# Wq's third row group by GpSimd's queue into the room of the first, Wk's second half in its place on the other two queues

## The chip, the core and the metric

The kernel runs on one core of a Trainium2 chip. The metric is the device time of one launch in microseconds, as the median of three runs. A core has five engines that matter here, each with an instruction queue that is worked off in order: TensorE (PE in the profile, with its weight loads as PEld), VectorE (DVE), ScalarE (ACT), GpSimd (POOL) and SyncE (SP), which only issues transfers. ScalarE and GpSimd can issue transfers (DMAs) as well. All arithmetic is in float32.

## The reference, cut to what matters

There are 32 graphs of 512 nodes with 512 features each, and two layers:

```python
h = relu(layernorm(x))                       # layer 0
agg = (adj @ h) / max(rowsum(adj), 1e-6)
x = x + relu(concat([h, agg]) @ W.T)
h = relu(layernorm(x))                       # layer 1
q, k = split(h @ Wqk, 2); v = h @ Wv
agg = adj @ (k * mask)
w = mask * sum(q * agg, -1) / sqrt(512)
x = x + softmax(w over the nodes)[:, None] * v
```

For layer 1, q is only ever multiplied with an aggregate of k. So the kernel computes the 512 x 512 product M = Wq Wk^T once, at its start, and uses h M in place of q and k. The change concerns how Wq and Wk, the two halves of `Wqk`, get into the core for this product.

## The kernel before, in words

The graphs are worked through one after the other in a loop; TensorE's 512 x 512 products are made with seven block products in place of eight (the lists `LEFT`, `RIGHT` and `ORDER`). The order of all instructions on each engine is written out by hand: the text of the kernel is the order of the queues (`tc.manual_schedule`), and a `Plan` says after which block product of TensorE other work is put.

The function `start` prepares the weights and the first graph. TensorE needs Wq and Wk transposed, and this is done in two steps. `exchange` loads a group of rows with four DMAs, one for each 32 partitions (in the order of `TURNS`), so that blocks of 32 x 32 come to lie in the right partitions; DVE's 32 x 32 transposition then does the rest (`turn_ordered` at line 769 for Wq, `turn_natural` at line 776 for Wk's first two groups, and a transposition written out at line 921 for Wk's second half). With `two_queues` the four DMAs of a group go by turns to SyncE's and ScalarE's queue; GpSimd issues none in `start`.

The pieces are:

- Wq comes in four groups of rows, `ask_wq(0)` to `ask_wq(3)`, each of 256 KB in four DMAs of 64 KB. Each lands in a room of its own in `sq`, a part of the tile `mv`, and `turn_wq(d)` transposes it into column d of `wqT` (a part of the tile `late`).
- Wk comes in two single groups, `ask_wk(0)` and `ask_wk(1)`, and its second half at once, `ask_wk(2, 2)`, in four DMAs of 128 KB. They land in `sk` and are transposed into `wkT`.
- `multiply(d, b, n)` is TensorE's part: row group d of Wq with n groups of Wk from b on. TensorE does them in the order (0, 0), (0, 1), (1, 0, 2), (2, 0, 2), then (0, 2, 2), (1, 2, 2), (2, 2, 2), and (3, 0, 2) and (3, 2, 2) around the first transpositions of the normalised x. Their rows carry the name `pm` and line 893.

DVE's order in `start` is: Wq's first rows, Wk's first and second group, Wq's second rows, Wq's third rows, Wk's second half in two pieces, Wq's fourth rows, and then the statistics of the first graph's x (line 266), each power of which is taken by GpSimd (line 272). GpSimd's own order before that is a few constants and `make_identity` (lines 197 and 199 of masks.py). Line 726 is GpSimd's only DMA in the kernel before: two loads of 512 KB for each graph that add to what lies there (names `tv<-dx`). In the profile the transfers of Wqk are `mv<-in_L_gnn_Wqk_dram`.

Of the kernel before, what the change touches and what calls it, by code (L numbers as in the profile page):

```python
# [22 lines left out]
def kernel(  # L23
# [11 lines left out]
    nc = tc.nc  # L35
# [181 lines left out]
    one_queue, two_queues = (nc.sync, nc.sync), (nc.sync, nc.scalar)  # L217
# [9 lines left out]
    def exchange(src, name, t=None, queues=one_queue):  # L227


        if t is None:  # L230
            t = big.tile([P, 8, P], F32, tag="s", bufs=2, name=name)
        for q in TURNS:
            queues[q // 2].dma_start(
                out=t[q * R:(q + 1) * R, :, :], in_=src[:, :, ts(q, P)].rearrange("k r j -> r k j")
            )
        return t
# [530 lines left out]
    def turn_ordered(t, d, dst, a, b):  # L767

        nc.vector.transpose(
            dst[:, a:b, ts(d, P)].rearrange("p a (k r) -> p k a r", r=R),  # L770
            t[:, :, a * R:b * R].rearrange("p k (a r) -> p k a r", r=R),
        )

    def turn_natural(t, h, dst, a, b):

        nc.vector.transpose(
            dst[:, a:b, ts(h, P)].rearrange("p a (k r) -> p k a r", r=R),
            t[:, :, a * R:b * R].rearrange("p k (a r) -> p k a r", r=R),
        )
# [37 lines left out]
    def start():  # L817
# [13 lines left out]
        def rows16(n):  # L831
            return room[:, n:n + 2048].rearrange("p (k f) -> p k f", f=P)

        sq, sk, s1 = rows16(0), rows16(2048), rows16(7168)
        wk_rows = weight_source(wqk[:, F:2 * F])
        wq_rows = wqk[:, 0:F].rearrange("(q c r) j -> c q r j", q=Q, c=C)
        def ask_wq(d):
            exchange(wq_rows[d], f"swq_{d}", sq[:, 4 * d:4 * d + 4], two_queues)

        def ask_wk(b, n=1):  # L840
            exchange(wk_rows[4 * b:4 * (b + n)], f"swk_{b}", sk[:, 4 * b:4 * (b + n)], two_queues)

        ask_wq(0)
        ask_wk(0)
        ask_wk(1)
        ask_wq(1)
        ask_wq(2)
        ask_wk(2, 2)
        ask_wq(3)
        room_x(0)  # L850
# [15 lines left out]
        wqT = late[:, 0:2048].rearrange("p (c f) -> p c f", c=C)  # L866
# [39 lines left out]

        def turn_wq(d, pieces=1):
            for a in range(pieces):
                turn_ordered(sq[:, 4 * d:4 * d + 4], d, wqT, 4 // pieces * a, 4 // pieces * (a + 1))

        def turn_wk(b, pieces=1):
            for a in range(pieces):
                turn_natural(sk[:, 4 * b:4 * b + 4], b, wkT, 4 // pieces * a, 4 // pieces * (a + 1))

        turn_wq(0)
        turn_wk(0, 2)
        turn_wk(1, 2)
        turn_wq(1, 2)
        turn_wq(2)
        for a in range(2):  # L920
            nc.vector.transpose(
# [159 lines left out]
        f = F1[0] = FrontH1(0)  # L1081
# [58 lines left out]
    }  # L1140
    with tc.manual_schedule(engines=engines):
        weights, mvR = start()
        post = None
        for i in range(1, B):
            more, last = i + 1 < B, i + 1 == B
            f = F1[i] = FrontH1(i)
# [240 lines left out]
```

## Time and profile before

| what | value |
|---|---|
| median of three runs | 2258.78 us (2258.16 to 2259.42) |
| profiled execution | 2258.43 us |
| its span, first to last instruction | 2256.7 us |
| instructions | 32841 |
| PE busy | 2251.1 us, 100% of the span |
| DVE busy | 1915.2 us, 85% |
| ACT busy | 1027.5 us, 46% |
| POOL busy | 176.1 us, 8% |
| data moved | 463.68 MB, 205 GB/s in the mean |

The profile is of one execution. "Busy" is the time in which at least one instruction of the engine ran. In lists of instructions a row gives the start and the length in us, the engine, the line of the kernel, the operation, the tile written and those read, how many instructions the row joins (x2), and in square brackets how long the engine was idle before them and what ended that: another engine's instruction, a DMA, or "issue" where the profile shows no cause. The chain of waits follows the work that ended last back to its start.

### The profile page before, as it was taken

Reading aid. Unit: us, or ns where it says so; the run is one execution under the profiler, and the core shown is the slowest. Engines: PE = TensorE matmul, PEld = TensorE weight load, DVE = VectorE, ACT = ScalarE, POOL = GpSimd, SP = SyncE. Lnnn points to the kernel's source line nnn. Section 1 sums busy time; section 2 is a strip of 40 time slices with the busy share of each in tenths; the row PEclk is TensorE's granted clock in tenths of the full one; section 3 lists DMA queues with packets and bytes.
Section 4 is the critical chain, followed back from the end, with each engine's and each line's share of the span. In section 5 each row is a group of like instructions: output and inputs, shape, how many; then the busy total and the mean of one; then the engine's idle time right before and its main releaser. Section 6 shows DMA issues by size and latency. Waiting matters only on the chain.

```text
span 2256.7 us, 32841 instructions
## 1 busy us (share of the span) xinstructions
PE 2251.1 (100%) x10532; PEld 1982.1 (88%) x10532; DVE 1915.2 (85%) x3786; ACT 1027.5 (46%) x1897; POOL 176.1 (8%) x261
## 2 busy tenths in 40 slices
PE   9999999999999999999999999999999999999999
PEld 7888888888888888888888888888888888888888
DVE  7998888888888888888888888888888888888787
ACT  5454443455434444434454344544444543445324
POOL 0000000000000000000001100000000000000000
PEclk9999999999999999999999999999999999999999
DMA  8878777777777786777777777777768777787543
GB/s 222 259 222 246 213 209 199 199 212 225 204 206 191 210 234 197 212 190 204 232 209 210 197 196 219 221 205 200 197 212 228 203 211 192 204 235 203 157 125 109
DMA packets 409150, 463.68 MB, mean 205 GB/s; under 512 B 37745, under 2 KB 271345, under 8 KB 404754
## 3 DMA queue, kind: packets, MB, share of 16 engines
q1 hardware_dynamic: 396914, 427.31, 63.7%
q0 software_dynamic: 8928, 32.51, 8.7%
q10 hardware_dynamic: 3136, 1.77, 0.3%
q8 instruction: 83, 1.36, 0.3%
q14 instruction: 89, 0.73, 0.1%
HBM read 293.93 MB, written 167.51 MB: 204 GB/s over the span
## 4 chain that ended last, share of the span: by engine, by line
PE 99%; DMA 0%; ACTq 0%; DVE 0%; issue 0%; DVEq 0%
PE ptv L498 28%; PE pp_o L105 20%; PE pp_y L105 10%; PE pp_u L105 10%; PE pq_o L105 10%; PE pq_y L105 5%; PE pr_o L105 5%; PE pq_u L105 5%; PE pr_u L105 2%; PE pr_y L105 2%; PE pw L549 1%; DMA mv<-in_L_gnn_Wqk_dram 0%; PE pm L893 0%; PE pp_t L105 0%; PE pp_v L105 0%; PE pq_v L105 0%
## 5 line engine op out<-in xcount | busy, mean ns | idle before, releaser
L498 PE MATMUL ptv<-mv,h1T 128*128 128x256 f32 x2842 | 618.1, 379 | 0.0
L498 PEld LDWEIGHTS ptv<-mv,h1T 128*128 128x128 f32 x2842 | 540.2, 190 | 73.2
L76 DVE TENSOR_TENSOR tv<-tv 128x256 f32<-128x256 f32 (+1 forms) x645 | 322.0, 511 | 13.2 <-ACT tv L82 1.5
L82 ACT ACTIVATE tv<-ptv 128x512 f32<-128x512 f32 (+1 forms) x360 | 185.2, 542 | 266.7 <-PE ptv L498 266.7
L105 PE MATMUL pp_u<-h1m,aT 128*128 128x256 f32 x1024 | 241.9, 379 | 0.0
L105 PE MATMUL pp_y<-wide 128*128 128x256 f32 x992 | 234.5, 379 | 0.0
L105 PE MATMUL pp_o<-y,aT 128*128 128x256 f32 x992 | 234.3, 379 | 0.0
L105 PE MATMUL pp_o<-w,wide 128*128 128x256 f32 x960 | 226.8, 379 | 0.0
L105 PEld LDWEIGHTS pp_u<-h1m,aT 128*128 128x128 f32 x1024 | 194.5, 190 | 26.4
L105 PEld LDWEIGHTS pp_o<-y,aT 128*128 128x128 f32 x992 | 188.5, 190 | 25.6
L105 PEld LDWEIGHTS pp_y<-wide 128*128 128x128 f32 x992 | 188.4, 190 | 25.7
L105 PEld LDWEIGHTS pp_o<-w,wide 128*128 128x128 f32 x960 | 182.5, 190 | 24.7
L82 ACT ACTIVATE o<-pp_o 128x512 f32<-128x512 f32 x96 | 57.3, 597 | 301.8 <-PE pp_o L105 301.8
L82 ACT ACTIVATE y<-pp_y 128x512 f32<-128x512 f32 x124 | 74.0, 597 | 231.7 <-PE pp_y L105 231.7
L76 DVE TENSOR_TENSOR tv<-ptv,tv 128x512 f32<-128x512 f32 x240 | 140.1, 615 | 44.4 <-PE ptv L498 40.3
L82 ACT ACTIVATE xu<-pp_u 128x512 f32<-128x512 f32 x127 | 75.8, 597 | 195.0 <-PE pp_u L105 195.0
L79 DVE TENSOR_TENSOR h1T<-h1T 128x512 f32<-128x512 f32 (+1 forms) x183 | 158.3, 879 | 1.2
L272 POOL TENSOR_TENSOR rstd<-rstd,mhalf 128x2 f32<-128x2 f32 (+1 forms) x97 | 79.9, 823 | 639.5 <-DVE rstd L271 639.5
L105 PE MATMUL pq_u<-h1m,aT 128*128 128x256 f32 x512 | 121.0, 379 | 0.0
L76 DVE TENSOR_TENSOR tv<-ptv,m_tv 128x512 f32<-128x512 f32 (+1 forms) x120 | 72.1, 622 | 56.5 <-PE ptv L498 55.6
L105 PE MATMUL pq_y<-wide 128*128 128x256 f32 x496 | 117.2, 379 | 0.0
L105 PE MATMUL pq_o<-y,aT 128*128 128x256 f32 x496 | 117.2, 379 | 0.0
(178 smaller groups left out, 3358.0 us busy)
## 6 DMA issues: line engine op xcount, KB each, us to landing
w<-dw SPq DMA_DIRECT2D x217, 256.0 KB, 4.2
dx<-xu SPq DMA_DIRECT2D x32, 1024.0 KB, 5.0
sh1T<-dh1T SPq DMA_DIRECT2D x256, 128.0 KB, 3.0
xu<-in_x_dram SPq DMA_DIRECT2D x124, 256.0 KB, 5.4
shT<-dhT SPq DMA_DIRECT2D x248, 128.0 KB, 4.8
daT<-a SPq DMA_DIRECT2D x124, 256.0 KB, 2.7
dh1T<-h1m SPq DMA_DIRECT2D x124, 256.0 KB, 3.2
tv<-dx POOLq DMA_DIRECT2D x62, 512.0 KB, 8.7
```

The lines of the kernel that those rows point to most:

```text
L76: (on or nc.vector).tensor_tensor(o, a, b, op=ALU.add)
L79: (on or nc.vector).tensor_tensor(o, a, b, op=ALU.subtract)
L82: nc.scalar.activation(o, i, AF.Copy)
L105: nc.tensor.matmul(p[:, rc, :], lt[:, LEFT[k], dk, ts(rc, P)], right[:, dk, :], start=first and rc == 0 and dk == 0, stop=True, skip_group ...
L272: nc.gpsimd.tensor_tensor(rstd[:, a:b], rstd[:, a:b], mhalf[:, a:b], op=ALU.pow)
L498: nc.tensor.matmul(banks[n][:, :, ts(i, P)], left[:, LEFT[k], LEFT_IN[j], :], mvR[:, RIGHT[k], RIGHT[j], :, :], start=first and i == 0, st ...
L549: nc.tensor.matmul(banks[n][:, ts(i, P)], left[:, LEFT[k], LEFT_IN[j], :], mvR[:, RIGHT[k], RIGHT[j], which, :], start=first and i == 0, s ...
```

## The change

Wq's third row group (d = 2) no longer has a room of its own: it is to land where the first group lay, `sq[:, 0:4]`. Its four DMAs leave the line of SyncE's and ScalarE's queues, and stand on GpSimd's queue instead, in the text after `turn_wq(0)`, since they may not overwrite the first group before it is transposed. On the other two queues Wk's second half and all that follows take the place that comes free. DVE's and TensorE's orders are as before.

```diff
-        def ask_wq(d):
-            exchange(wq_rows[d], f"swq_{d}", sq[:, 4 * d:4 * d + 4], two_queues)
+        wq_room = {d: sq[:, n:n + 4] for d, n in ((0, 0), (1, 4), (2, 0), (3, 12))}
+
+        def ask_wq(d, queues=two_queues):
+            exchange(wq_rows[d], f"swq_{d}", wq_room[d], queues)
...
         ask_wk(0)
         ask_wk(1)
         ask_wq(1)
-        ask_wq(2)
         ask_wk(2, 2)
         ask_wq(3)
...
         def turn_wq(d, pieces=1):
             for a in range(pieces):
-                turn_ordered(sq[:, 4 * d:4 * d + 4], d, wqT, 4 // pieces * a, 4 // pieces * (a + 1))
+                turn_ordered(wq_room[d], d, wqT, 4 // pieces * a, 4 // pieces * (a + 1))
...
         turn_wq(0)
+        ask_wq(2, (nc.gpsimd, nc.gpsimd))
         turn_wk(0, 2)
         turn_wk(1, 2)
         turn_wq(1, 2)
```

## The prediction

> **What bounds the kernel now.** I read the page first, then the busy time by stretches. The columns are length, PE, PE's weight loads, DVE, ACT, POOL (each busy us and count), PE's granted clock, DMA share, GB/s.
>
> ```profile
> PE 2251.1 (100%) x10532; PEld 1982.1 (88%) x10532; DVE 1915.2 (85%) x3786; ACT 1027.5 (46%) x1897; POOL 176.1 (8%) x261
> ...
> 0.00:12.46 12.46, 10.15 (x36) 6.59 (x36) 5.04 (x12) 1.49 (x2) 0.68 (x6) 1.00 0.69 184
> 12.46:2253.40 2240.94, 2240.91 (x10496) 1975.53 (x10496) 1909.78 (x3774) 1025.98 (x1895) 175.44 (x255) 1.00 0.73 206
> ```
>
> From 12.46 to 2253.40 PE is idle for 0.03 us in all. Whatever moves the point at 12.46 moves the end by as much: nothing later can absorb a delay, and nothing later can be gained. The change touches only what lies before 12.46, so I need the chain and the two feeding engines there.
>
> ```profile
> 4.87 2.93 DMA mv<-in_L_gnn_Wqk_dram
> ...
> 7.82 3.69 DMA mv<-in_L_gnn_Wqk_dram
> ...
> 11.70 0.72 DVE late L921
> ...
> 12.46 7.17 PE pm L893 x32
> ```
>
> The chain says start, length, what. The last piece of Wk's second half lands at 11.51 (7.82 + 3.69); 0.19 us later DVE's transposition of it starts, and 0.76 us after that start PE begins its 32 dense products. One block product of eight takes 7.17 / 4 = 1.79 us. Now DVE's, PE's and POOL's instructions in order of time (start, length, engine, line):
>
> ```profile
> 7.99 0.77 DVE L769 STREAM_TRANSPOSE late<-mv 128x256 f32<-128x256 f32 x2 [0.93 <-DMA mv<-in_L_gnn_Wqk_dram]
> 9.13 0.71 DVE L769 STREAM_TRANSPOSE late<-mv 128x512 f32<-128x512 f32 x1 [0.37 <-DMA mv<-in_L_gnn_Wqk_dram]
> 11.70 1.30 DVE L921 STREAM_TRANSPOSE late<-mv 128x512 f32<-128x512 f32 x2 [1.86 <-DMA mv<-in_L_gnn_Wqk_dram]
> ...
> 8.49 3.72 PE L893 MATMUL pm<-late 128*128 128x256 f32 x16 [0.30 <-DVE late L769]
> ...
> 8.44 0.28 POOL masks.py:199 TENSOR_SCALAR_AFFINE_SELECT late<-late 128x128 f32<-128x128 f32 x1 [7.51 <-issue]
> 15.66 0.74 POOL L272 TENSOR_TENSOR rstd<-rstd,mhalf 128x2 f32<-128x2 f32 x1 [6.94 <-DVE rstd L271]
> ```
>
> The three DVE rows are Wq's second rows, Wq's third rows and Wk's second half. PE's 16 from 8.49 are `multiply(1, 0, 2)` and `multiply(2, 0, 2)`; the second needs Wq's third rows and starts near 8.49 + 1.79 = 10.28. POOL's first real work, the identity matrix, starts only at 8.44, after 7.51 us that the profile ascribes to nothing visible, and POOL's queue is in order.
>
> **The change part by part.** *Two DMAs fewer on each of SyncE's and ScalarE's queues* before Wk's second half. The transpositions at 7.99 and 9.13 each waited for one 256 KB group, so a group passes in 1.14 us, and Wk's second half may land 1.14 us sooner, at 10.37. The later loads on SyncE's queue move up likewise; they are not what ends anything here (the first statistics follow the transpositions without a wait). ScalarE is freed some 0.9 us earlier; its next work that PE needs is at 16.22, so that is worth nothing. The naming of rooms costs nothing.
>
> *Four DMAs of 64 KB on GpSimd's queue.* Their wait for the room, the first transposition (3.90 + 0.71 = 4.61), is over long before POOL comes to them: ahead of them stands the identity, done at 8.44 + 0.28 = 8.72. What is queued behind them on POOL is the power at 15.66, whose input will itself be late. The price of such a DMA has to come from the one kind that the trace has on this queue, the 512 KB accumulating loads of line 726, of the same 128 rows to describe but 4 KB instead of 512 B in each:
>
> ```profile
> L726 POOL DMA_DIRECT2D tv<-dx x62: 861/966/1177, 161.2 to 2239.4; - x62
> ...
> DMA to landing us min/median/max: 5.7/8.7/10.9
> ...
> 231.91 0.86 POOL L726 DMA_DIRECT2D tv<-dx  x1 [0.17 <-issue]
> ...
> mv<-in_L_gnn_Wqk_dram SPq DMA_DIRECT2D x12, 64.0 KB, 2.6
> ```
>
> Issue: 0.966 + 0.17 gap = 1.14 us each, so the fourth begins at 8.72 + 3 x 1.14 = 12.14 (ends: 0.89 to 1.35 us each, from 0.861 back to back and 1.177 + 0.17). From its issue to its landing the trace gives bounds alone: 2.6 us for 64 KB on the other queue, 5.7 us for the shortest load of this queue, with eight times the bytes. I take 3.54, nearer the lower: the software queue's first packet comes 2.4 us after the first issue at 161.21 (the DMA view of 161.2 to 163.6 has no packet of it, that of 161.2 to 164 has three), and 256 KB pass in 1.14. So Wq's third rows land at 15.68, in place of about 8.94 (9.13 less 0.19).
>
> The Trainium skill, DMA: Bandwidth & Descriptors (Anatomy of one DMA), fits a DMA of this path as 2.0 us plus bytes over 436 GB/s, an estimate of 2.15 us for 64 KB; line 726 is well above the 3.2 us it gives for 512 KB. By it the landing would be at 14.29 and the forecast 1.39 us lower. The same page (its table of what to do) says that spreading DMAs over SP, ACT and GpSimd brings no bandwidth, which speaks against the change; no run here shows it yet.
>
> *The wait on DVE.* `turn_wq(2)` keeps its place in DVE's order. Behind it stand Wk's second half, Wq's fourth rows and the statistics of x: all wait for the late rows, although Wk's half lies there from about 10.4. PE waits with its ninth to sixteenth product. DVE starts at 15.68 + 0.19 = 15.87, PE at 15.87 + 0.76 = 16.63, and after 1.79 us stands, at 18.42, where it now stands at 12.46. That is 5.96 us. The old wait for Wk's half is gone within it: DVE turns that in 0.7 us while PE works on the 1.79 us product. Next in line is DVE's chain to the first normalised x; it moves by 15.87 + 0.71 - 11.70 = 4.9 us, less than PE does, so PE's own order still ends last.
>
> *The clock.* PE will stand still from about 10.3 to 16.6, 6.3 us. The trace shows the granted clock falling after PE has been mostly idle, and slow products at the start (equal stretches of 1.20 us):
>
> ```profile
> 2252.79:2256.20 3.41, 0.58 (x6) 0.39 (x4) 0.88 (x3) 0.00 (x0) 0.00 (x0) 1.00 0.49 154
> 2256.20:2256.70 0.50, 0.00 (x0) 0.00 (x0) 0.00 (x0) 0.00 (x0) 0.00 (x0) 0.50 0.00 0
> ...
> 5.54:6.74 1.20, 1.20 (x5) 1.20 (x6) 0.72 (x3) 0.00 (x0) 0.00 (x0) 1.00 0.71 173
> 6.91:8.11 1.20, 1.20 (x12) 1.08 (x10) 0.27 (x2) 0.00 (x0) 0.00 (x0) 1.00 0.87 256
> ```
>
> PE's last product ends at 2253.4; by 2256.2 the clock is 0.50. So 6.3 us of rest should lose it too. At the start products ran at about half pace from 1.48 to some 6.8, although the column has 1.00 there already (it knows no earlier record). A second such stretch would lose half of 5.3, 2.67 us; a clock that holds would lose 0. No gain is possible, as the clock is 1.00 now. I take 2.0, nearer the upper end, since it is the same engine coming out of a rest.
>
> The Trainium skill, TensorE: Matmul & The Clock Gate (Part 1), puts both the fall and the return at about 3.4 us of rest or of work, in windows that run freely. By it the loss would be an estimate of 1.7 us or somewhat more.
>
> **The sum.** 5.96 + 2.0 = 7.96 us. The profiled execution took 2258.43, 1.73 over its span of 2256.7 and 0.35 under the median 2258.78. It becomes 2266.4, and the median 2258.78 + 7.96 = 2266.7. By the low ends: landing at 8.72 + 3 x 0.89 + 2.6 = 13.99, delay 13.99 + 0.95 + 1.79 - 12.46 = 4.27, no clock loss: 2263.0. By the high ends: landing at 8.72 + 3 x 1.35 + 5.7 = 18.47, delay 8.75, clock 2.67: 2270.2.
>
> **The rivals.** *The rows come late, the clock holds.* For it: the kernel shows one fall only, at its end. Against: that fall came after less rest. 2258.78 + 5.96 = 2264.7.
>
> *Not slower: GpSimd's DMAs come in time.* It needs the fourth piece landed by 12.46 - 1.79 - 0.95 = 9.72; from there on the change costs. Then Wk's half starts DVE at 10.56 instead of 11.70, but PE is not done with its 16 products before 8.49 + 2 x 1.79 = 12.07, so 0.39 us is all: 2258.4. Against it: POOL is free 1.0 us before 9.72, and one 64 KB load alone takes 2.6 on SyncE's queue. Even if the DMAs could go out at 4.61, ahead of the identity, the landing would be at 4.61 + 3.42 + 3.54 = 11.57 and the loss 1.85: 2260.6.
>
> *GpSimd's queue is as slow as its slowest row.* With 10.9 us to land: 8.72 + 4.05 + 10.9 = 23.67, delay 13.95, clock 2.0: 2274.7. For it: these are its first DMAs, among SyncE's loads of x and W0. Against: 64 KB is an eighth of what that row moved.
>
> **How the numbers follow.** Late with a cold clock 0.76, late with a warm one 0.12, in time or nearly 0.06, slowest row 0.06. The range 2263.0 to 2270.2 holds the first two and leaves out the others and their edges. What a measurement here can tell from no change is 0.2%, 4.5 us. Slower than 2263.3 by the first and fourth cases and most of the second: 0.92; within 4.5 us: 0.07; faster by 4.5 us has no mechanism: 0.01.
>
> **What would show it.** Right: POOL's row at 8.44 followed by four issues, DVE idle 5 us or more before the third-rows transposition with the DMA as releaser, PE's 40 products starting near 16.6, some at half pace with a clock record of 0.5, then PE idle nowhere as before. Wrong: issues on POOL before 8.4, a transposition before 13, a PE that rests under 3 us, or PE gaps after 20 us, which would mean that a later stage pays.

## The result and the profile after

The changed kernel takes 2266.78 us (median of six runs, 2266.54 to 2268.37) where the kernel before takes 2258.73 (six runs, 2258.16 to 2259.42): 8.05 us more, a ratio of 1.0037 with a 95% interval of 1.0024 to 1.0050. The forecast was 2266.7, slower by 7.96. The span of the profiled execution went from 2256.7 to 2264.9.

The page's first rows show where to look: PE has the same 10532 products and is no longer the whole span.

```profile
PE 2252.8 (99%) x10532; PEld 1982.8 (88%) x10532; DVE 1914.6 (85%) x3786; ACT 1027.7 (45%) x1897; POOL 180.1 (8%) x265
```

Now the changed kernel's instructions in order of time, engine by engine (start, length, what, and in brackets the idle time before and what ended it): POOL, DVE and PE.

```profile
8.42 0.28 POOL masks.py:199 TENSOR_SCALAR_AFFINE_SELECT late<-late 128x128 f32<-128x128 f32 x1 [7.49 <-DMA mv<-in_L_gnn_Wqk_dram]
8.68 2.53 POOL L233 DMA_DIRECT2D mv<-in_L_gnn_Wqk_dram  x4
...
8.44 0.77 DVE L769 STREAM_TRANSPOSE late<-mv 128x256 f32<-128x256 f32 x2 [1.43 <-DMA mv<-in_L_gnn_Wqk_dram]
16.75 0.71 DVE L769 STREAM_TRANSPOSE late<-mv 128x512 f32<-128x512 f32 x1 [7.54 <-DMA mv<-in_L_gnn_Wqk_dram]
17.38 1.26 DVE L923 STREAM_TRANSPOSE late<-mv 128x512 f32<-128x512 f32 x2
...
8.94 1.99 PE L894 MATMUL pm<-late 128*128 128x256 f32 x8 [0.66 <-DVE late L769]
17.51 10.48 PE L894 MATMUL pm<-late 128*128 128x256 f32 x40 [6.58 <-DVE late L769]
27.83 1.04 PE L802 MATMUL h<-late,h 128*128 128x128 f32 x8
```

The identity still starts at 8.42, and the four DMAs follow at 8.68. DVE stands idle for 7.54 us before the third rows (16.75) and then takes Wk's second half without any wait (17.38), since it has been there for long. PE has its first eight products from 8.94, rests for 6.58 us, and does 40 in a row from 17.51. The row of the identity names a DMA as what ended its 7.49 us of idling; that the DMA did so is not shown, for the same silence stands as "issue" in the kernel before (7.51) and in e1 (7.89). The 40 take 10.48 us, more than five times the 1.79 us of a block product. The chain of waits (start, length) says what the rest consists of:

```profile
8.42 0.28 POOL late masks.py:199
8.70 0.85 POOL mv L233
...
9.56 1.09 POOL mv L233 x2
10.65 5.97 DMA mv<-in_L_gnn_Wqk_dram
```

The fourth DMA is issued at 10.65 and lands at 16.62, 5.97 us later. The busy time by stretches (columns as in the prediction; the granted clock, 1.00 at full speed, is the third from the right) explains the slow products:

```profile
10.52:13.93 3.41, 0.41 (x2) 0.01 (x1) 0.00 (x0) 0.00 (x0) 0.68 (x2) 1.00 0.86 240
13.93:17.34 3.41, 0.00 (x0) 0.00 (x0) 0.59 (x1) 0.00 (x0) 0.00 (x0) 0.50 1.12 263
17.34:20.76 3.42, 3.25 (x8) 2.60 (x9) 3.35 (x8) 0.00 (x0) 0.00 (x0) 0.50 1.22 239
20.76:24.17 3.41, 3.41 (x18) 3.00 (x17) 2.40 (x9) 0.00 (x0) 0.97 (x2) 1.00 1.06 334
20.40:2261.50 2241.10, 2241.10 (x10499) 1975.17 (x10497) 1906.89 (x3770) 1026.24 (x1895) 176.97 (x255) 1.00 0.72 205
```

The clock falls to half at 13.93 and comes back at 20.76. From 17.51 to 20.76 PE works at half pace: 3.25 us, of which 1.62 are lost. After that PE is never idle, as before. So the start of the first transposition of x on PE (line 802) is a good meter of the whole loss. In the kernel before it is at 19.48, in the changed one at 27.83, 8.35 later:

```profile
19.48 1.04 PE L802 MATMUL h<-late,h 128*128 128x128 f32 x8
```

From that row to PE's last product both traces take 2233.90 us. What follows PE's last product, the stores of the end, took 2.9 to 4.3 us in the profiles of this study; there, and in the scatter of single runs, the meter and the medians part.

### The profile page after: what moved, and what is told of

It is laid out like the page before. It is cut to its first block, busy times and chain, and to the rows that moved or that the text cites. A ratio compares the mean times of both kernels' runs of the same rounds, so it can differ in the third digit from the quotient of the medians.

```text
span 2264.9 us, 32846 instructions
## 1 busy us (share of the span) xinstructions
PE 2252.8 (99%) x10532; PEld 1982.8 (88%) x10532; DVE 1914.6 (85%) x3786; ACT 1027.7 (45%) x1897; POOL 180.1 (8%) x265
## 4 chain that ended last, share of the span: by engine, by line
PE 99%; DMA 1%; POOL 0%; DVE 0%; issue 0%; DVEq 0%
PE ptv L498 28%; PE pp_o L105 20%; PE pp_y L105 10%; PE pp_u L105 10%; PE pq_o L105 10%; PE pq_y L105 5%; PE pq_u L105 5%; PE pr_o L105 5%; PE pr_y L105 2%; PE pr_u L105 2%; PE pw L549 1%; DMA mv<-in_L_gnn_Wqk_dram 1%; PE pm L894 1%; PE pp_t L105 0%; PE pp_v L105 0%; PE pq_v L105 0%
```

## The experiments

Theory A is the prediction's: the loss is the lateness of the third rows, at the place where DVE's and PE's orders need them, plus what PE's clock loses in the rest. By its sum a landing at time T shifts the meter by T + 0.95 + 1.79 - 12.46 = T - 9.72: 0.95 us from the landing to PE's first product with the third rows, 1.79 for that block product, and 12.46 is where PE now starts its dense stretch. Two rivals were that GpSimd's queue is slow whenever it is used (B), and that the other order or the traffic of a third queue costs in itself (C). The medians stand against those of the kernel before taken on the same chip: 2258.51 for e1, e2, e3 and e5, 2258.49 for e4, e6, e7 and e8, 2258.65 for e9 and e10. Every run also has a mean granted clock, to three digits. A stretch of 3.41 us at half clock takes 0.0008 off the mean of some 2258 us, so a run with a mean of 1.000 had no such stretch behind its slow start, which the clock's record does not hold.

**e1: the identity behind the DMAs.**

```diff
-        make_identity(nc, identity)
...
         ask_wq(2, (nc.gpsimd, nc.gpsimd))
+        make_identity(nc, identity)
```

> The changed kernel with one line moved: the identity matrix stands behind the four GpSimd DMAs instead of ahead of them, so that they can go out when the first transposition is done, near 4.65 us. Theory A (the loss is the lateness of Wq's third rows, most of it the identity ahead of the DMAs): the fourth DMA is issued near 6.6, lands 3.5 to 6.0 us later at 10.1 to 12.6, so PE's delay is landing less 9.72 = 0.4 to 2.9 us, and PE rests too little for its clock to fall: 2259.1 to 2261.6. Theory B (GpSimd's queue is slow whenever it is used, about 8 us from its first issue to its last landing as in the changed kernel): landing at 12.6, 2261.6 at the least. Theory C (the loss comes from other traffic or from Wk's half going first, not from the identity): no change, near 2266.8.

Measured: 2260.73, ratio 1.0010 (1.0001 to 1.0019), 2.22 us over the kernel before, where the changed kernel has 8.05. POOL in order of time, the chain, PE, and the stretches:

```profile
4.98 2.44 POOL L233 DMA_DIRECT2D mv<-in_L_gnn_Wqk_dram  x4 [4.54 <-DMA mv<-in_L_gnn_Wqk_dram]
7.39 0.25 POOL masks.py:197 MEMSET late<- 128x128 f32 x1
15.52 0.28 POOL masks.py:199 TENSOR_SCALAR_AFFINE_SELECT late<-late 128x128 f32<-128x128 f32 x1 [7.89 <-issue]
...
6.85 5.20 DMA mv<-in_L_gnn_Wqk_dram
...
12.94 8.90 PE pm L893 x40
...
21.68 1.04 PE L802 MATMUL h<-late,h 128*128 128x128 f32 x8
...
8.91:12.33 3.42, 1.99 (x8) 1.44 (x8) 0.55 (x3) 1.29 (x2) 0.00 (x0) 1.00 0.92 204
12.33:15.74 3.41, 2.80 (x13) 2.49 (x14) 2.45 (x4) 0.00 (x0) 0.22 (x1) 1.00 0.58 171
```

The landing is at 12.05, so theory A's shift is 2.33; the meter's row in PE's list is at 21.68, a shift of 2.20. The 7 to 8 us without visible cause go with the identity (7.89 now), not with the DMAs. So 5.83 of the 8.05 us, the clock's part among them, were the place of the DMAs in GpSimd's order. Of theory B something is left: 5.20 us from the last issue to the landing, here beside what SyncE and ScalarE load of Wqk (issued until 8.68), for x is issued only at 12.17. C is out for the main part. The clock held in this profile, but not in every run: seven of the eleven have a mean of 1.000 and took 2259.78 to 2261.02 us, four have 0.999 and took 2261.86 to 2262.24, some 1.7 us more, as one stretch at half clock costs. No profile shows one of those four.

**e2: the third rows first on GpSimd's queue, in their own room.**

```diff
-        make_identity(nc, identity)
...
-        wq_room = {d: sq[:, n:n + 4] for d, n in ((0, 0), (1, 4), (2, 0), (3, 12))}
+        wq_room = {d: sq[:, n:n + 4] for d, n in ((0, 0), (1, 4), (2, 8), (3, 12))}
...
+        ask_wq(2, (nc.gpsimd, nc.gpsimd))
+        make_identity(nc, identity)
         ask_wq(0)
         ask_wk(0)
...
         turn_wq(0)
-        ask_wq(2, (nc.gpsimd, nc.gpsimd))
```

> The changed kernel with Wq's third rows in a room of their own again and their four GpSimd DMAs as the first work of that queue, ahead of the identity. They go out near 0.75 us. Theory A: they land before 9.72 (0.75 + 2.0 for the issues + 3.5 to 6 = 6.2 to 8.7), the loss is gone, and Wk's half going earlier is worth at most 0.4 us: 2258.3 to 2258.8. Theory B (the queue itself costs): they land late even so, over 9.72, and the time is 2260 or more. Theory C (Wk's half going first, or the third queue's traffic, costs in itself): over 2260 although the rows are early.

Measured: 2259.99 (2258.66 to 2261.69), ratio 1.0005 (0.9997 to 1.0014). Theory A's number is missed by 1.2 us. DVE and PE in order of time, then the stretches:

```profile
8.02 0.77 DVE L776 STREAM_TRANSPOSE late<-mv 128x256 f32<-128x256 f32 x2 [1.68 <-DMA mv<-in_L_gnn_Wqk_dram]
8.87 1.36 DVE L769 STREAM_TRANSPOSE late<-mv 128x256 f32<-128x256 f32 x3
...
8.52 13.03 PE L895 MATMUL pm<-late 128*128 128x128 f32 x56 [1.29 <-DVE late L776]
21.39 1.04 PE L802 MATMUL h<-late,h 128*128 128x128 f32 x8
...
4.84:8.26 3.42, 1.43 (x9) 0.97 (x8) 1.02 (x3) 0.00 (x0) 0.00 (x0) 1.00 0.70 176
8.26:11.67 3.41, 3.15 (x12) 2.88 (x13) 1.89 (x5) 1.49 (x2) 0.28 (x1) 0.50 1.02 237
```

The third rows are no longer waited for: the second and third rows are turned in one go at 8.87. But 256 KB more ahead of the first pieces make Wk's second group late, 8.02 in place of 6.29 in the kernel before:

```profile
6.29 0.77 DVE L776 STREAM_TRANSPOSE late<-mv 128x256 f32<-128x256 f32 x2 [0.48 <-DMA mv<-in_L_gnn_Wqk_dram]
```

PE rests for it, and its clock is at half from 8.26 to 11.67. The gain that the rows' earliness should bring went there: C holds for early traffic. In six of the eleven runs the mean clock is 1.000, so it did not fall; their median of 2259.2 is still 0.7 us above the kernel before.

**e3: products of zeros in PE's rest.**

```diff
+        for n in range(7):
+            nc.tensor.matmul(spare, still[:, 0:P], still, start=True, stop=True)
         multiply(2, 0, 2)
```

> The changed kernel with seven more products of zeros on TensorE (128x512, 0.86 us each) between multiply(1, 0, 2) and multiply(2, 0, 2), where it waits; nothing reads them. Theory A: they fill 10.8 to 16.8, the granted clock stays 1.0, and the 1.6 us that the half clock costs are given back: 2265.2. Rival: the half clock is hidden behind another wait and nothing changes: 2266.8. If the fill is too long it adds its excess.

Measured: 2265.19, ratio 1.0029 (1.0017 to 1.0040), 6.68 us over the kernel before. PE:

```profile
10.09 6.17 PE L947 MATMUL spare<-late 128*128 128x512 f32 x14
17.27 8.90 PE L894 MATMUL pm<-late 128*128 128x256 f32 x40 [1.01 <-DVE late L769]
26.01 1.04 PE L802 MATMUL h<-late,h 128*128 128x128 f32 x8
```

The same 40 products take 8.90 in place of 10.48 us: the clock's part is real and is 1.58 us (1.37 between the medians, 8.05 less 6.68). The landing of this profile, at 16.38 by its chain, gives a shift of 6.66 without any loss by the clock; the meter moved by 6.53.

**e4: nothing else on the wires.** The wires are the 16 DMA engines. The loads of x, W0 and adj move from ahead of the first transposition to behind the third rows and the small DMA:

```diff
         ask_wq(3)
-        room_x(0)
...
         turn_wq(0)
         ask_wq(2, (nc.gpsimd, nc.gpsimd))
+        seen = dram.tile([P, 16], F32, tag="seen", bufs=1, name="seen")
+        nc.sync.dma_start(out=seen, in_=wq_room[2][:, 3, 0:16])
+        room_x(0)
...
```

> The changed kernel with SyncE's queue held back: a small DMA that reads the room of Wq's third rows stands ahead of the loads of x, W0 and adj, so that these go out only when the third rows have landed. Its time is worse by what x comes later; the question is how long the four GpSimd DMAs take. In the changed kernel the last one took 5.97 us from issue to landing, and the four 7.94 us from the first issue. Theory A1 (they share the DMA engines with the loads of x and W0): with those gone the last lands 2.5 to 3.6 us after its issue, near 13.2 to 14.3. Theory A2 (the software queue is that slow by itself): 5.5 to 6 us again, near 16.5.

Measured, in one run: 2262.59. The chain, PE, the DMA view (queue, count, size, median us to landing), where the changed kernel has 5.1 for the same four, and the stretches:

```profile
10.65 2.11 DMA mv<-in_L_gnn_Wqk_dram
...
13.65 10.43 PE L879 MATMUL pm<-late 128*128 128x256 f32 x40 [3.24 <-DVE late L769]
23.92 1.04 PE L802 MATMUL h<-late,h 128*128 128x128 f32 x8
...
mv<-in_L_gnn_Wqk_dram POOLq DMA_DIRECT2D x4, 64.0 KB, 2.2
...
9.95:13.36 3.41, 0.47 (x3) 0.06 (x1) 0.47 (x1) 0.00 (x0) 1.25 (x3) 1.00 0.30 81
13.36:16.78 3.42, 3.13 (x7) 2.50 (x8) 2.02 (x4) 0.00 (x0) 0.00 (x0) 0.50 0.69 143
```

Issued at the same 10.65, the last piece lands after 2.11 us instead of 5.97. The 3.9 us between them come with SyncE's loads of x and W0 (adj is issued behind the landing in the changed kernel, at 17.10); A1 holds. The share of the DMA engines that is busy tells the same: 0.30 from 9.95 to 13.36 here, 0.86 and 1.12 in the two stretches from 10.52 of the changed kernel. With these loads held back the kernel is 4.1 us over the kernel before instead of 8.05, although x then comes late. The shift of the meter is 4.44; by the sum it is 12.76 - 9.72 = 3.04, and half of the 3.13 us that PE worked at half clock, 4.61 together.

**e5: Wk's half ahead of the third rows, both on the old queues.**

```diff
-        ask_wq(2)
         ask_wk(2, 2)
+        ask_wq(2)
```

> The kernel before with one pair of lines swapped: Wk's second half goes ahead of Wq's third rows on the same two queues, each in its own room, GpSimd as before; DVE and TensorE keep their order. Theory A: the third rows land last, at 11.5 us, where Wk's half lands now, so the delay is 11.51 - 9.72 = 1.8 us: 2260.5. Rival (Wk's half earlier is worth something in itself): 2258.4. Rival (the order alone is what costs in the change): near 2266.

Measured: 2259.88, ratio 1.0006 (0.9997 to 1.0014), 1.37 over the kernel before. DVE, PE, and the stretch with the rest:

```profile
11.32 0.71 DVE L769 STREAM_TRANSPOSE late<-mv 128x512 f32<-128x512 f32 x1 [2.50 <-DMA mv<-in_L_gnn_Wqk_dram]
...
20.82 1.04 PE L802 MATMUL h<-late,h 128*128 128x128 f32 x8
...
10.44:13.86 3.42, 1.88 (x9) 1.60 (x9) 2.49 (x4) 1.46 (x2) 0.00 (x0) 1.00 0.73 184
```

The rows land at 11.12 by the chain (0.4 sooner than expected), which gives 1.40; the meter moves by 1.34. So one half of the change, Wk's half first, is a loss even without GpSimd. The interval reaches below 1, but all eleven runs (2259.41 to 2260.33) lie above the highest of the kernel before (2259.29).

**e6: the shared room alone.** The kernel before with the changed kernel's rooms; what SyncE and ScalarE load from the third rows on stands in the text behind the first transposition, in the same order:

```diff
-            exchange(wq_rows[d], f"swq_{d}", sq[:, 4 * d:4 * d + 4], two_queues)
+            exchange(wq_rows[d], f"swq_{d}", wq_room[d], queues)
...
         turn_wq(0)
+        ask_wq(2)
+        ask_wk(2, 2)
+        ask_wq(3)
```

> The kernel before with only the room shared: Wq's third rows land where the first lay, but on the same two queues and in the same place of their order. The wait for the first transposition, which ends at 4.6, stands at DMAs that are issued from 5.05 on. Theory A: no change, 2258.5. Rival (the wait for the room is what holds the queues up): one or more us slower, since Wk's half stands behind it.

Measured: 2258.58, ratio 1.0001 (0.9991 to 1.0010). The room shows no cost, as the prediction had it.

**e7: DVE and PE take the third rows last.**

```diff
-        turn_wq(2)
...
         variance(t, 0, 2)
+        turn_wq(2)
...
-        multiply(2, 0, 2)
-        for d in range(3):
-            multiply(d, 2, 2)
+        multiply(0, 2, 2)
+        multiply(1, 2, 2)
...
+        multiply(3, 0, 2)
+        multiply(3, 2, 2)
...
+        multiply(2, 0, 2)
...
+        multiply(2, 2, 2)
```

> The changed kernel with its loads as they are, but DVE and TensorE taking what is there: Wk's half, Wq's fourth rows and the first two statistics stand ahead of the third rows on DVE, and TensorE does its products with the third rows last. Theory A (the loss is the order of DVE and TensorE behind a late landing): TensorE starts near 11.2 on Wk's half, has 4 x 1.79 us of other products, until 18.4, and finds the third rows turned (landing 16.6 + 0.95): the first x is turned 0.5 us later than in the kernel before, the clock stays up: 2259.1. Rival (the traffic of the third queue delays everything): 2262 or more.

Measured: 2259.20, ratio 1.0004 (0.9995 to 1.0012). DVE and PE:

```profile
10.47 1.31 DVE L922 STREAM_TRANSPOSE late<-mv 128x512 f32<-128x512 f32 x2 [1.80 <-DMA mv<-in_L_gnn_Wqk_dram]
16.77 0.71 DVE L769 STREAM_TRANSPOSE late<-mv 128x512 f32<-128x512 f32 x1 [0.57 <-DMA mv<-in_L_gnn_Wqk_dram]
...
11.23 8.90 PE L894 MATMUL pm<-late 128*128 128x256 f32 x40 [0.84 <-DVE late L922]
19.97 1.04 PE L802 MATMUL h<-late,h 128*128 128x128 f32 x8
```

All transfers are those of the changed kernel, and the third rows are turned as late as there (16.77). Yet all but 0.71 of the 8.05 us are gone, because what PE needs next no longer stands behind them. This is the clearest verdict: the loss was the orders of DVE and PE behind a late landing.

**e8: the third rows last, but on the old queues.** The loads of x, W0 and adj move behind them:

```diff
-        ask_wq(2, (nc.gpsimd, nc.gpsimd))
+        ask_wq(2)
+        room_x(0)
...
```

> The changed kernel with the third rows in the same room and behind Wk's half and Wq's fourth rows, but by SyncE's and ScalarE's queues in place of GpSimd's, ahead of x. Theory A: the last pieces land where Wq's fourth rows land now, near 12.1, so the delay is 12.07 - 9.72 = 2.4 us: 2260.9; what is left of the loss, about 6 us, is GpSimd's own (its start at 8.7, its landings, the clock). Rival (coming last is what costs, whatever the queue): near 2266.

Measured: 2263.07 (2261.25 to 2264.29), ratio 1.0019 (1.0010 to 1.0028); 2.2 us over theory A's number. DVE and PE, then the stretches:

```profile
12.28 0.71 DVE L769 STREAM_TRANSPOSE late<-mv 128x512 f32<-128x512 f32 x1 [3.32 <-DMA mv<-in_L_gnn_Wqk_dram]
...
13.05 10.59 PE L879 MATMUL pm<-late 128*128 128x256 f32 x40 [2.36 <-DVE late L769]
23.47 1.04 PE L802 MATMUL h<-late,h 128*128 128x128 f32 x8
...
11.00:14.41 3.41, 1.36 (x6) 1.23 (x7) 2.13 (x4) 0.92 (x2) 0.00 (x0) 1.00 0.83 229
14.41:17.83 3.42, 3.42 (x9) 2.71 (x9) 2.46 (x8) 0.00 (x0) 0.74 (x1) 0.50 1.09 270
```

The landing is where it was expected (12.09, a shift of 2.37). The rest of PE is only 2.36 us, and still the clock falls, at 14.41, after a stretch in which PE was 40% busy. That costs 1.71 and makes 4.08; the meter moved by 3.99. The forecast had no clock loss for so short a rest. In the other runs it went both ways: six of the eleven, this one among them, have a mean clock of 0.999 and took 2263.07 to 2264.29; five have 1.000 and took 2261.25 to 2262.33. The fall costs some 1.5 us between the medians of the two groups; the five without it, with a median of 2261.89, are still 1.0 over theory A's number.

**e9: e8 with two products of zeros in the rest.**

```diff
+        for n in range(2):
+            nc.tensor.matmul(spare, still[:, 0:P], still, start=True, stop=True)
         multiply(2, 0, 2)
```

> e8_two_queues_last took 2263.1 where 2260.9 was expected, and its clock record shows half pace from 14.4 to 17.8 after a rest of TensorE of only 2.4 us. This kernel adds two products of zeros (128x512, 0.86 us each, nothing reads them) into that rest, ahead of multiply(2, 0, 2). Theory A (the rows come 2.4 us late, and the rest is the clock): the clock stays at 1.0 and the time is 2260.9. Rival (the late loads of x or another wait make up the rest): 2263 again.

Measured: 2261.77 (2261.38 to 2262.23), ratio 1.0013 (1.0004 to 1.0022): between the two expectations, and near the 2261.89 of e8's runs without a fall. The mean clock is 1.000 in all eleven. PE:

```profile
13.33 8.90 PE L879 MATMUL pm<-late 128*128 128x256 f32 x40 [0.48 <-DVE late L769]
22.07 1.04 PE L802 MATMUL h<-late,h 128*128 128x128 f32 x8
```

The 40 products take 8.90 again, the landing is at 12.37, and the meter moves by 2.59 where the sum gives 2.65. What is left, 0.5 us of the median, lies behind the meter, where this profile has a tail of some 4.3 us against 3.3 in the kernel before. Why, stays open.

**e10: e2 with one product of zeros.**

```diff
+        nc.tensor.matmul(spare, still[:, 0:P], still, start=True, stop=True)
         multiply(0, 1)
```

> e2_early_own_room took 2260.0 where 2258.3 to 2258.8 was expected; its trace shows Wk's second group 1.7 us later than in the kernel before, TensorE resting for it, and half pace from 8.3 to 11.7. This kernel adds one product of zeros (128x512) into that rest, ahead of multiply(0, 1). Theory A (the miss is the clock): the clock stays up, TensorE has its products done about when it has them in the kernel before, and the time is 2258.3 to 2258.8. Rival (the early traffic of the third queue costs by the later rows themselves): 2260 again.

Measured: 2259.08 (2258.38 to 2260.46), ratio 1.0003 (0.9994 to 1.0012). In the profile the clock holds and the 56 products from 8.70 take 11.53 us in place of 13.03:

```profile
8.70 11.53 PE L895 MATMUL pm<-late 128*128 128x128 f32 x56 [0.70 <-DVE late L776]
20.07 1.04 PE L802 MATMUL h<-late,h 128*128 128x128 f32 x8
```

So e2's miss is the clock for 1.3 us of its meter. Wk's second group is late all the same, and the meter is still 0.59 later than in the kernel before. The runs lie in two groups, near 2258.6 and near 2260.2. The clock does not explain them: of the five runs from 2259.96 up four have a mean of 1.000, and only the slowest has 0.999. What does stays open.

No version tried beats the kernel before. The medians that come closest, of e6, e10 and e7, are 0.1 to 0.7 us above it.

## Why the prediction was right, point by point

The mechanism was right. The size was right to 0.1 us in the medians, and that is luck: three terms were off, by 1.49 too much, 2.43 too little and 0.38 too much, and partly made up for each other. With the measured terms the sum is 6.84 + 1.62 = 8.46, the meter moved by 8.35, and single runs of one kernel differ by more than 1 us.

- *No slack behind 12.46.* Right: from the meter to PE's last product it is 2233.90 us before and after.
- *GpSimd's order decides when the DMAs go out.* Right, 8.68 against 8.72. e1 shows it by itself: 5.83 us.
- *Issue.* Mis-sized: four at 1.14 us were assumed from the accumulating loads of line 726; the chain shows 0.85 for the first and 0.55 for each of the others. The fourth began at 10.65, not 12.14: 1.49 too much.
- *Landing.* Mis-sized the other way: 3.54 assumed, 5.97 measured, which lies even above the high end of 5.7. The failed step is the 1.14 us for passing 256 KB, a pace read where only Wqk's own loads were under way (in the kernel before, x is issued from 10.23 on). The 2.4 us to the first packet was no measure either: in e4 the whole DMA took 2.11. I had named the loads of x and W0 beside them in a rival only. e4 measures what they add: 3.86.
- *The landing in sum.* 15.68 against 16.62, and so 5.96 against 6.84 for the delay without the clock (17.51 + 1.79 - 12.46).
- *The two prices of the DMA page.* The Trainium skill, DMA: Bandwidth & Descriptors (Anatomy of one DMA), gave an estimate of 2.15 us. The quiet wires of e4 agree, with 2.11; the changed kernel does not, with 5.97. The page's formula has no term for other traffic. Its advice that a third issuing engine brings no bandwidth agrees with e2: 256 KB more from GpSimd made Wk's second group 1.7 us late.
- *The order of DVE and PE.* Right; e7 removes the loss by changing it alone. Wk's half was there at 10.3 in e7, as foreseen (10.37).
- *The clock.* Right in kind; 2.0 assumed, 1.62 by the trace and 1.58 by e3. The Trainium skill, TensorE: Matmul & The Clock Gate (Part 1), gave an estimate of 1.7 or somewhat more, nearer than mine. On what makes the clock fall, the page asks for an idle window of about 3.4 us. Here a stretch of that length that was still 40% busy was enough, with a rest of 2.36 us, in the profile of e8.
- *The rivals.* The one that was not slower needed a landing by 9.72. e5, e8 and e9 bear that point out: landings at 11.12, 12.09 and 12.37 moved the meter by what they exceed it, to 0.1 us, the clock aside. Its other part, that the DMAs sent ahead of the identity would still lose, holds too: 1.85 us forecast, 2.22 measured in e1. The warm one, late rows and a clock that holds, is what e3 makes: 5.96 us forecast, 6.68 measured, for the landing was later than assumed. The slowest row was far off: 10.9 us to land, 5.97 measured.

## What to carry to other kernels

Before a transfer is moved to another engine's queue, read what stands ahead of it on that queue, and what is queued behind its consumer on the engines that work in order; here the first was an identity matrix of 0.28 us with 7.5 us of silence before it, and the second was the whole start of the kernel. A row for the same kind of transfer gives its price only beside the same traffic. And if a rest on TensorE can't be avoided, put the work that is there into it (e7), or count half of the slow stretch that follows as part of the price.

## What was not expected of the hardware

- The four GpSimd DMAs of 64 KB landed a median 2.2 us after issue on quiet wires and 5.1 beside SyncE's loads of x and W0.
- Within a profile, the changes of TensorE's granted clock lie 3.41 us or a multiple of it apart. Counted in such stretches, the clock fell after ones in which PE was 40% (e8) and 42% (e2) busy. It held in the profiles of e1 and e5, where the rests were 1.92 and 1.54 us and the emptiest such stretch was 58% and 55% busy. The same kernel can go either way: as far as mean and time tell, it fell in six of eleven runs of e8, in five of e2, in four of e1 and in none of e5.
- The silence before GpSimd's identity was 7.1 to 8.1 us wherever it stood: 7.10 in e10, 7.31 in e2, 7.49 in the changed kernel, 7.89 in e1, 8.11 in e5.
